# Selective scan over 128 x 128 pixels: middle-group rows stored in turn, and the carried state added to the first token instead of being the scan's initial value

## The chip, the cores and the metric

One core of one Trainium2 chip. The metric is the device time of one execution in microseconds (us); the time before is the median of three runs. Where a profile is read, it is that of one profiled execution, whose own time stands beside it.

## The reference, cut to what matters

Two images of 96 channels and 128 x 128 pixels go through a layer norm, a four-directional selective scan (Mamba), a feed-forward part with 8-bit rounding, a 3 x 3 convolution and a second feed-forward part. Nearly all the time goes to the scan, which for each of four pixel orders (rows, rows backwards, columns, columns backwards) computes:

```python
xz = x @ in_w.T
xc, z = jnp.split(xz, 2, axis=-1)            # 192 channels each
xc = silu(causal_conv4(xc) + conv_b)
xdbl = xc @ xproj_w.T                        # dt (6), B (16), C (16) per token
dt = softplus(dt_raw @ dt_w.T + dt_b)
A = -jnp.exp(A_log)                          # 192 channels x 16 states
# for every token, in order:
dA = jnp.exp(dt_t[:, :, None] * A)
h = dA * h + dt_t[:, :, None] * B_t[:, None, :] * u_t[:, :, None]
y = jnp.einsum('bds,bs->bd', h, C_t)
# then
y = (y + Dp * xc) * silu(z)
out = y @ outp_w.T                           # and a fusion of the four orders
```

## The kernel before, in words

For each image, `normalize` writes the normed image to DRAM once by rows (`xnr`) and once by columns (`xnc`). `mamba` then does the scans, and `ffn_and_conv` the rest.

**Tiling of the scan.** Two pixel orders are worked together as a pair (`PAIRS`: rows with columns, then the two backward ones). 2 x 192 channels make three groups `g` of 128 partitions. Group 1, the middle one, holds the last 64 channels of the first order on partitions 0 to 63 and the first 64 of the second order on 64 to 127. The 16384 tokens are cut into 32 pieces of 512 (`T`). A pair and a piece are a step (`pi`, `i`): 64 steps per image, 128 in all. A step has 24 units: three groups times eight pairs of states (`s`, `s + 1`). A unit `k` is handled in turn `k` of one loop (L436), which writes out the order of every engine's instructions by hand:

- `fetch` (L386) loads, every second turn, B rows six turns and C rows four turns ahead (`B_AHEAD`, `C_AHEAD`), on SyncE's queue (SP). `row_tile` (L312) copies each row from DRAM to all partitions of the group: 1 MB a tile in one transfer, but for the middle group in two of 512 KB, 64 partitions each, since the two orders have different rows.
- `feed` (L391) multiplies the B rows with dt times u on GpSimd (`b_part`, L324), two units ahead; `feed_decay` makes `exp(dt A)` on ScalarE into PSUM (`decay`, L330), two units ahead.
- `scan` (L334) runs the recurrence on VectorE, one instruction per state, written over the decay in PSUM. Its initial value is the number 0 in a first piece (`i == 0`), else a column of `hst`. The order within a turn is: first scan of unit k, `behind(k - 1)`, second scan of unit k.
- `behind` (L403) multiplies with the C rows on VectorE (L409), copies the last state to `hst` on ScalarE (L410), and sums over states on TensorE into PSUM `y` (`sums`, L341). When a group begins, the `y` of the last one is gated (`gated`, L349, VectorE).
- The next step's `prologue` (L210) is spread over the turns by a list `at` (L301) of turn, place in the turn and function: input loads in turn 0, input convolutions on TensorE in turns 4, 5 and 6 with ScalarE taking the results in the same turns (L233), the gates in 7, 10 and 11, silu of xc at the end of turn 8 and of sz at the end of turn 14 (`silu`, L244, with a table load on either side), the B, C and dt rows in turn 12, from where they are stored to DRAM (L261). The softplus of each group starts in turns 13, 18 and 21 and takes four GpSimd operations (L287, L290, L293, L297).
- `project` and `collect` (L352, L361) apply the output weights (`gmat`) four turns after a group ends, that is, in turn 3 of the next step for the last group.

All engines keep this order; SP's transfers wait in it too, each for the buffer that it writes. A B tile has four buffers, a C tile three, the decay three.

`_layout` (L566) rearranges the weights on the host.

Of the kernel before, what the change touches and what calls it, by code (L numbers as in the profile page):

```python
# [10 lines left out]
F32 = mybir.dt.float32  # L11
# [9 lines left out]
C = 96  # L21
# [21 lines left out]
def tile_metaformer(ctx: ExitStack, tc: tile.TileContext, a: dict, out: bass.AP):  # L43
# [34 lines left out]
    inx = cpool.tile([C, 4, 4, DI], F32, name="inx")  # L78
    nc.vector.memset(gmat, 0.0)
    with tc.tile_pool(name="prep", bufs=1) as pp, tc.tile_pool(name="prep_ps", bufs=2, space=PSUM) as pps:  # L80
        alog = pp.tile([128, 2, NG, S], F32, name="alog")
        nc.sync.dma_start(alog, a["alog"])
        nc.scalar.activation(alog, alog, AF.Exp)
        nc.vector.tensor_scalar_mul(amat, alog, -1.0)

        dskip = pp.tile([128, 2, NG], F32, name="dskip")
        nc.sync.dma_start(dskip, a["dskip"])
        for pi in range(2):
            for g in range(NG):
                nc.vector.tensor_scalar_mul(dmat[:, pi, g, :], ident, dskip[:, pi, g : g + 1])  # L90

        inxw = pp.tile([C, 4, DI], F32, name="inxw")
        nc.sync.dma_start(inxw, a["inx"])
        taps = pp.tile([C, 4, 4, DI], F32, name="taps")
        nc.sync.dma_start(taps, a["taps"].broadcast_to((C, 4, 4, DI)))
        for d in range(4):
            nc.vector.tensor_tensor(inx[:, d], taps[:, d], inxw[:, d, None, :].broadcast_to((C, 4, DI)), ALU.mult)
        outw = pp.tile([C, 4, DI], F32, name="outw")
        nc.sync.dma_start(outw, a["outw"])
        fusew = pp.tile([C, 4, C], F32, name="fusew")  # L100
        nc.sync.dma_start(fusew, a["fusew"])
        for pi, (da, db) in enumerate(PAIRS):

            pieces = [
                (slice(0, 128), da, 0, 128),
                (slice(0, 64), da, 128, 192),
                (slice(64, 128), db, 0, 64),
                (slice(0, 128), db, 64, 192),
            ]
            for g, (rows, d, lo, hi) in enumerate(pieces):  # L110
                ps = pps.tile([128, C], F32, name="ps")
                nc.tensor.matmul(ps[rows, :], outw[:, d, lo:hi], fusew[:, d, :], start=True, stop=True)
                nc.vector.tensor_copy(gmat[rows, pi, g, :], ps[rows, :])

# [68 lines left out]
    def mamba(acc, xnr, xnc):  # L183

        with ExitStack() as st:
# [4 lines left out]

            hst = one.tile([128, NG, S], F32, name="hst")
            acc_w = acc.rearrange("c (h w) -> c w h", w=W)

# [16 lines left out]
            def prologue(pi, i, d):  # L210
# [19 lines left out]
                def conv_out(g):  # L230
                    if g == 0:
                        d["xc"] = two.tile([128, NG, T], F32, name="xc")
                    nc.scalar.activation(d["xc"][:, g, :], d["ps"], AF.Identity, bias=convb[:, pi, g : g + 1])  # L233

# [3 lines left out]
                def gate_out(g):  # L238
                    if g == 0:
                        d["sz"] = two.tile([128, NG, T], F32, name="sz")  # L240
                    nc.scalar.copy(d["sz"][:, g, :], d["ps"])

# [12 lines left out]
                def rows_out():  # L255

                    d["rows"] = one.tile([BCO + NBC, T], F32, name="rows")
                    nc.scalar.copy(d["rows"], d["ps"][0 : BCO + NBC, :])
                    d["bcd"] = rows_d.tile([COPIES, 2, NBC // 2, T], F32, name="bcd")
                    for n in range(COPIES):  # L260
                        nc.sync.dma_start(d["bcd"][n].rearrange("k r t -> (k r) t"), d["rows"][BCO:, :])  # L261
# [39 lines left out]
                at = [(0, 0, load), (8, 1, partial(silu, "xc")), (14, 1, partial(silu, "sz"))]  # L301
                at += [(12, 0, rows), (12, 1, rows_out)]
                for g, k in enumerate((4, 5, 6)):
# [8 lines left out]
            def row_tile(d, g, s, k, ahead):  # L312

                t = gen.tile([128, 4, T], F32, name=f"row{k}", bufs=ahead + 1)
                for half in range(2) if g == 1 else (slice(None),):
                    rows = slice(half * 64, half * 64 + 64) if g == 1 else half
                    at = s + S * (half if g == 1 else g // 2)
                    n = (64 if g == 1 else 128) // COPIES
                    src = d["bcd"][None, :, k, at : at + 4, :].broadcast_to((n, COPIES, 4, T))
                    nc.sync.dma_start(t[rows], src)  # L320
                return t

            def b_part(d, g, b):
                nc.gpsimd.tensor_tensor(b, d["dtu"][g][:, None, :].broadcast_to((128, 2, T)), b, ALU.mult)  # L324

            def decay(pi, d, g, s):
# [5 lines left out]

            def scan(i, g, s, j, da, b, h):
                nc.vector.tensor_tensor_scan(  # L334
                    h[:, j, :], da[:, j, :], b[:, j, :],
                    0.0 if i == 0 else hst[:, g, s + j : s + j + 1], ALU.mult, ALU.add,
                )

# [52 lines left out]
            def feed(k):  # L391
                if k < total:
                    n = k // nu
                    b_part(state[n], units[k % nu][0], bs[k])

# [40 lines left out]
            for k in range(total + 6):  # L436
                n, u = divmod(k, nu)
                if u == 0 and n + 1 < len(steps):
                    for m, where, f in prologue(*steps[n + 1], state[n + 1]):
                        later(k + m, where, f)  # L440
                if k % 2 == 0:
                    fetch(k + 2 * B_AHEAD, 0, B_AHEAD, bs)
                feed(k + AHEAD)
                issue(k, 0)
                if k < total:
                    (_, i), (g, s) = steps[n], units[u]
                    da, b = das.pop(k), bs.pop(k)
                    hs[k] = b if (g, s) in BY_POOL else da
                    scan(i, g, s, 0, da, b, hs[k])
                if 0 < k <= total:  # L450
                    behind(k - 1)
                if k < total:
                    scan(i, g, s, 1, da, b, hs[k])
                if k % 2 == 0:
# [111 lines left out]
def _layout(v):  # L566

    f = np.float32
    order = [d for pair in PAIRS for d in pair]
    rows = lambda w: w[order].reshape(2, NG, 128, -1).transpose(2, 0, 1, 3)  # L570
    xw = v["L0_conv_xproj_w"]
    bcw = np.zeros((2, 2 * DI, BCO + NBC), f)
    dtw = np.zeros((2 * RK, 2, 2 * DI), f)
    for pi, pair in enumerate(PAIRS):
        for k, d in enumerate(pair):
# [5 lines left out]
            dtw[k * RK : (k + 1) * RK, pi, at] = v["L0_conv_dt_w"][d].T  # L581
    grouped = lambda w: w.reshape(2, NG, 128, -1).transpose(2, 0, 1, 3)
    out = {
# [4 lines left out]
        "taps": v["L0_conv_conv_w"].transpose(0, 2, 1)[None],  # L588
        "convb": rows(v["L0_conv_conv_b"])[..., 0],
        "bcw": grouped(bcw),  # L590
        "dtw": dtw,
        "dtb": rows(v["L0_conv_dt_b"])[..., 0],
        "alog": rows(v["L0_conv_A_log"]),
        "dskip": rows(v["L0_conv_Dp"])[..., 0],
        "outw": v["L0_conv_outp_w"].transpose(1, 0, 2),
        "fusew": v["L0_conv_fuse_w"].reshape(C, 4, C).transpose(2, 1, 0),
# [26 lines left out]
```

## Time and profile before

| | |
|---|---|
| median of three runs | 13000.71 us (12998.91 to 13001.96) |
| profiled execution | 13004.29 us, span of its core 13002.5 us |
| granted TensorE clock, mean | 0.963 of full speed |
| VectorE scans (L334) | 6144 of some 1.27 us, 7565 us busy |
| GpSimd B multiplies (L324) | 3072 of 2.36 us, 7176 us busy |
| ScalarE decays (L330) | 6144 of 0.69 us, 4249 us busy |
| TensorE sums over states (L341) | 12288 passes, 6120 us busy |
| VectorE C multiplies (L409) | 3072 of 1.21 us, 3706 us busy |
| transfers | 3400 MB, 262 GB/s over the span |

The profile is one execution, recorded by the chip. Each row of instruction groups gives line, engine, operation, the tiles that it writes and reads with their shapes, and the count; then busy time in us, the mean duration of one in ns, and how long the engine stood idle just before them, with what ended that idle time. In rows in order of time the first number is the start in us, the second the duration of the merged instructions, and brackets hold the idle time before them and what ended it. TensorE is PE (PEld its weight loads), VectorE DVE, ScalarE ACT, GpSimd POOL, SyncE's queue SPq. The releaser in brackets is inferred; where several things were waited for, only the last is named.

### The profile page before, as it was taken

The page shows a single profiled execution, that of the slowest core. Times are in us where ns is not written, and L with a number is a line of the kernel's source. Part 1 is how long each engine was busy: PE and PEld are TensorE (multiplying, and loading weights), DVE is VectorE, ACT ScalarE, POOL GpSimd, SP SyncE. Part 2 cuts the span into 40 slices and gives each one's busy share as a digit, 9 for nine tenths or more (in the row PEclk, how much of TensorE's full clock was granted, in tenths as well). Part 3 has the DMA queues.
Part 4 walks back from the last instruction along what each step waited for, and adds up shares of the span by engine and source line. Part 5 has one row for each costly group of instructions (what it writes and reads, how often), then busy time and mean ns, then how long its engine had stood idle before and what let it go on. Part 6 is the DMA issues. An engine that isn't in the chain of part 4 may idle for free. (4 is left out here: it accounts for less than half of the span.)

```text
span 13002.5 us, 97992 instructions
## 1 busy us (share of the span) xinstructions
PE 10850.3 (83%) x24208; PEld 3987.1 (31%) x24208; DVE 11569.1 (89%) x10865; ACT 8560.0 (66%) x14738; POOL 9215.4 (71%) x4772
## 2 busy tenths in 40 slices
PE   6888888888888888888978888888888888888889
PEld 2323233333333333333323333332333333333233
DVE  5999999999999999995459999999999999999954
ACT  6666666666666666665566666666666666666655
POOL 4877778777787787772147778777787777877721
PEclk8999999999999999999989999999999999999999
DMA  7999999999999999992079999999999999999920
GB/s 226 287 294 282 298 288 285 295 283 298 288 285 295 283 295 289 285 295 68 13 226 285 298 283 292 290 285 298 285 291 291 284 298 286 290 294 281 296 61 13
DMA packets 545331, 3400.40 MB, mean 262 GB/s; under 512 B 81612, under 2 KB 82732, under 8 KB 146840
## 3 DMA queue, kind: packets, MB, share of 16 engines
q1 hardware_dynamic: 544760, 3394.12, 83.1%
q8 instruction: 195, 3.19, 0.1%
q14 instruction: 376, 3.08, 0.1%
HBM read 3288.94 MB, written 104.86 MB: 261 GB/s over the span
## 5 line engine op out<-in xcount | busy, mean ns | idle before, releaser
L324 POOL TENSOR_TENSOR row<-dtu,row 128x1024 f32<-128x1024 f32 x3072 | 7175.7, 2358 | 1739.3 <-DMA row<-bcd 1419.2
L334 DVE TENSOR_TENSOR_SCAN da<-da,hst,row 128x512 f32<-128x512 f32 x5952 | 7339.4, 1274 | 351.2 <-ACT da L330 194.6
L341 PE MATMUL y<-row,ident 128*128 128x512 f32 x12288 | 6120.1, 626 | 1113.3 <-DVE row L409 1098.9
L330 ACT ACTIVATE da<-dt,amat 128x512 f32<-128x512 f32 x6144 | 4249.4, 692 | 207.5 <-ACT hst L410 0.4
L341 PEld LDWEIGHTS y<-row,ident 128*128 128x128 f32 x12288 | 2288.9, 197 | 4779.4 <-DVE row L409 2292.3
L409 DVE TENSOR_TENSOR row<-da,row 128x1024 f32<-128x1024 f32 x3072 | 3705.9, 1206 | 19.6 <-DMA row<-bcd 18.8
L410 ACT COPY hst<-da 128x2 f32<-128x2 f32 x3072 | 484.0, 158 | 2235.5 <-DVE row L409 2233.3
L416 PE MATMUL y<-xc,dmat 128*128 128x512 f32 x768 | 526.1, 773 | 779.1 <-DVE sz L349 779.1
L287 POOL TENSOR_TENSOR q<-e,q 128x512 f32<-128x512 f32 x384 | 488.0, 1271 | 821.8 <-ACT hst L410 709.1
L233 ACT ACTIVATE xc<-misc,convb 128x512 f32<-128x512 f32 x384 | 264.2, 688 | 1117.5 <-PE misc L207 1117.5
L207 PE MATMUL misc<-xa,inx 96*128 96x512 f32 (+1 forms) x2048 | 932.4, 597 | 59.0 <-DMA xa<-xnr 57.2
L207 PE MATMUL misc<-xb,inx 96*64 96x512 f32 (+1 forms) x2048 | 928.1, 595 | 1.6 <-ACT xc L233 1.6
L531 POOL TENSOR_TENSOR acc<-acc,y 96x512 f32<-96x512 f32 x128 | 147.6, 1153 | 987.0 <-DVE y L530 987.0
L541 PE MATMUL pc<-pad,kw 96*96 96x512 f32 x1152 | 566.7, 593 | 0.0
L207 PEld LDWEIGHTS misc<-xa,inx 96*128 96x128 f32 (+1 forms) x2048 | 323.6, 163 | 625.5 <-issue 493.4
L293 POOL TENSOR_TENSOR dt<-dt,ln 128x512 f32<-128x512 f32 x384 | 486.9, 1268 | 30.1
L297 POOL TENSOR_TENSOR dtu<-dt,xc 128x512 f32<-128x512 f32 x384 | 488.5, 1272 | 0.5
L290 POOL TENSOR_TENSOR ln<-ln,q 128x512 f32<-128x512 f32 x384 | 488.1, 1271 | 0.5
L359 PE MATMUL misc<-sz,gmat 128*96 128x512 f32 x1024 | 483.6, 594 | 0.0
L416 PEld LDWEIGHTS y<-xc,dmat 128*128 128x128 f32 x768 | 129.0, 211 | 1102.1 <-DVE sz L349 1099.1
L268 PE MATMUL misc<-rows,dtw 12*128 12x512 f32 x768 | 439.7, 652 | 18.5 <-ACT dt L275 17.2
L132 DVE TENSOR_TENSOR xq<-xm,rs 96x512 fp8e5<-96x512 f32 x128 | 87.9, 687 | 387.8 <-ACT rs L128 387.8
(75 smaller groups left out, 8403.8 us busy)
## 6 DMA issues: line engine op xcount, KB each, us to landing
row<-bcd SPq DMA_DIRECT2D x2048, 1024.0 KB, 7.5
row<-bcd SPq DMA_DIRECT2D x2048, 512.0 KB, 8.0
bcd<-rows SPq DMA_DIRECT2D x512, 128.0 KB, 9.8
xa<-xnr SPq DMA_DIRECT2D x124, 193.1 KB, 5.8
xb<-xnc SPq DMA_DIRECT2D x124, 193.1 KB, 5.5
acc<-in_x_dram SPq DMA_DIRECT2D x16, 768.0 KB, 17.8
xnr<-xn SPq DMA_DIRECT2D x16, 768.0 KB, 4.3
xnc<-stg SPq DMA_DIRECT2D x16, 768.0 KB, 5.6
```

The source lines that it names most:

```text
L207: nc.tensor.matmul(ps[rows, :], w(PAIRS[pi][d], k, lo, hi), src[d][:, k : k + T], **se)
L287: nc.gpsimd.tensor_tensor(d["q"], d["e"], d["q"], ALU.subtract)
L290: nc.gpsimd.tensor_tensor(d["ln"], d["ln"], d["q"], ALU.add)
L293: nc.gpsimd.tensor_tensor(d["dt"][g], d["dt"][g], d["ln"], ALU.add)
L297: nc.gpsimd.tensor_tensor(dtu, d["dt"][g], d["xc"][:, g, :], ALU.mult)
L324: nc.gpsimd.tensor_tensor(b, d["dtu"][g][:, None, :].broadcast_to((128, 2, T)), b, ALU.mult)
L330: nc.scalar.activation(da[:, j, :], d["dt"][g], AF.Exp, scale=amat[:, pi, g, s + j : s + j + 1])
L334: nc.vector.tensor_tensor_scan(h[:, j, :], da[:, j, :], b[:, j, :], 0.0 if i == 0 else hst[:, g, s + j : s + j + 1], ALU.mult, ALU.add,)
L341: nc.tensor.matmul(y, ident, c[:, j, :], start=False, stop=s + j == S - 1)
L409: nc.vector.tensor_tensor(c, h, c, ALU.mult)
L416: nc.tensor.matmul(y, dmat[:, pi, g, :], d["xc"][:, g, :], start=True, stop=False)
L541: nc.tensor.matmul(pc, kw[:, t, :], rows, start=t == 0, stop=t == 8)
```

## The change

Three things are changed.

**Rows of the middle group in turn.** In group 1 the 64 channels of the first order now lie on the even partitions and those of the second on the odd ones. `row_tile` writes every second partition in each of its two transfers. TensorE still produces the two halves on partitions 0 to 63 and 64 to 127; ScalarE takes them into a tile of their own (`mixed`), and two transfers of 64 x 512 elements each (`mix`), issued on SP, move them to every second row of `xc` (turn 7) and of `sz` (turn 12). The silu of turns 8 and 14 reads what they wrote. The weights are rearranged to match, those for the output with zero rows in between (`outx`), so that `gmat` needs no memset.

**The state enters through the first token.** All scans start from the number 0. Instead, for steps with `i > 0`, `entering` makes `exp(dt A)` of a group's first token for its 16 states on ScalarE and multiplies it with `hst` on GpSimd (128 x 16), at the end of turn 20 for group 0, and of turns 4 and 12 of the step itself for groups 1 and 2. `b_part` then adds two of these values to the first tokens of the unit's B tile, an operation of 128 x 2 elements on GpSimd after the multiply.

**Row stores later.** The copies of the B and C rows to DRAM are issued at the start of turn 14 instead of the end of turn 12 (`rows_to_dram`).

```diff
                 def conv_out(g):
                     if g == 0:
                         d["xc"] = two.tile([128, NG, T], F32, name="xc")
-                    nc.scalar.activation(d["xc"][:, g, :], d["ps"], AF.Identity, bias=convb[:, pi, g : g + 1])
+                    t = mixed("xc") if g == 1 else d["xc"][:, g, :]
+                    nc.scalar.activation(t, d["ps"], AF.Identity, bias=convb[:, pi, g : g + 1])
...
-                    nc.scalar.copy(d["sz"][:, g, :], d["ps"])
+                    nc.scalar.copy(mixed("sz") if g == 1 else d["sz"][:, g, :], d["ps"])
+
+                def mixed(name):
+                    d["mix", name] = one.tile([128, T], F32, name=f"mix_{name}")
+                    return d["mix", name]
+
+                def mix(name):
+
+                    for k in range(2):
+                        nc.sync.dma_start(d[name][k:128:2, 1, :], d["mix", name][64 * k : 64 * k + 64, :])
...
-                at += [(12, 0, rows), (12, 1, rows_out)]
+                at += [(12, 0, rows), (12, 1, rows_out), (14, 0, rows_to_dram)]
+                at += [(7, 0, partial(mix, "xc")), (12, 0, partial(mix, "sz"))]
...
-                    rows = slice(half * 64, half * 64 + 64) if g == 1 else half
+
+                    rows = slice(half, 128, 2) if g == 1 else half
...
-            def b_part(d, g, b):
+            def entering(pi, d, g):
+
+                nc.scalar.activation(enter[:, g, :], amat[:, pi, g, :], AF.Exp, scale=d["dt"][g][:, 0:1])
+                nc.gpsimd.tensor_tensor(enter[:, g, :], enter[:, g, :], hst[:, g, :], ALU.mult)
+
+            def b_part(i, d, g, s, b):
                 nc.gpsimd.tensor_tensor(b, d["dtu"][g][:, None, :].broadcast_to((128, 2, T)), b, ALU.mult)
+                if i > 0:
+                    nc.gpsimd.tensor_tensor(b[:, :, 0], b[:, :, 0], enter[:, g, s : s + 2], ALU.add)
...
-            def scan(i, g, s, j, da, b, h):
-                nc.vector.tensor_tensor_scan(
-                    h[:, j, :], da[:, j, :], b[:, j, :],
-                    0.0 if i == 0 else hst[:, g, s + j : s + j + 1], ALU.mult, ALU.add,
-                )
+            def scan(j, da, b, h):
+                nc.vector.tensor_tensor_scan(h[:, j, :], da[:, j, :], b[:, j, :], 0.0, ALU.mult, ALU.add)
...
                     for m, where, f in prologue(*steps[n + 1], state[n + 1]):
                         later(k + m, where, f)
+                    if steps[n + 1][1] > 0:
+                        for g in range(NG):
+                            later(k + nu - 4 + nu // NG * g, 1, entering, steps[n + 1][0], state[n + 1], g)
```

## The prediction, made before the changed kernel ran

> **What bounds the kernel now.** I read the engine totals first, then busy time by stage, then the groups with shapes kept apart, then VectorE, GpSimd, ScalarE and SyncE in order of time through one step. The chain of waits is no help: it covers only the last few per cent. The two scan stages (168 to 5936 us and 6650 to 12427 us) hold 11,545 of the 13,002 us; each is 64 steps of 24 units, so a step takes some 90 us.
>
> ```profile
> PE 10850.3 (83%) x24208; PEld 3987.1 (31%) x24208; DVE 11569.1 (89%) x10865; ACT 8560.0 (66%) x14738; POOL 9215.4 (71%) x4772
> ...
> row<-bcd SPq DMA_DIRECT2D x2048, 1024.0 KB, 7.5
> row<-bcd SPq DMA_DIRECT2D x2048, 512.0 KB, 8.0
> ```
>
> VectorE leads. The 512 KB transfers (half a middle-group tile) take as long to land as whole tiles. By stretches (PE, PEld, DVE, ACT, POOL busy, then clock, DMA share, GB/s):
>
> ```profile
> 2924.00:2934.00 10.00, 6.19 (x13) 2.04 (x13) 9.76 (x9) 9.56 (x14) 2.65 (x2) 1.00 1.00 388
> 2984.00:2994.00 10.00, 10.00 (x29) 4.13 (x26) 8.51 (x8) 4.34 (x9) 6.39 (x4) 1.00 0.82 197
> ```
>
> Middle-group transfers move half the bytes per second. The second stretch is also one where PE is full and VectorE is not. The scans, by shape:
>
> ```profile
> L334 DVE TENSOR_TENSOR_SCAN da<-da,hst,row 128x512 f32<-128x512 f32 x5952 | 7339.4, 1274 | 351.2 <-ACT da L330 194.6 <-ACT hst L410 134.2 <-issue 21.2
> ...
> L334 DVE TENSOR_TENSOR_SCAN da<-da,row 128x512 f32<-128x512 f32 x192 | 225.6, 1214 | 180.9 <-POOL row L324 170.9 <-ACT hst L410 5.2 <-ACT da L330 4.7
> ```
>
> The 192 scans of the four first steps already take a constant as initial value: 60 ns shorter. One step, VectorE:
>
> ```profile
> 2990.84 1.28 DVE L334 TENSOR_TENSOR_SCAN da<-da,hst,row 128x512 f32<-128x512 f32 x1
> 2993.61 1.29 DVE L334 TENSOR_TENSOR_SCAN da<-da,hst,row 128x512 f32<-128x512 f32 x1 [1.49 <-ACT da L330]
> ...
> 3024.90 1.29 DVE L334 TENSOR_TENSOR_SCAN da<-da,hst,row 128x512 f32<-128x512 f32 x1 [1.27 <-ACT hst L410]
> ```
>
> A unit (two scans, one multiply) repeats every 3.486 us; a gating (L349) adds 0.6. Twice per step VectorE waits for ScalarE: at unit 9 and at unit 17. GpSimd, ScalarE and SyncE around these:
>
> ```profile
> 3023.38 1.27 POOL L287 TENSOR_TENSOR q<-e,q 128x512 f32<-128x512 f32 x1 [5.28 <-ACT hst L410]
> ...
> 3061.60 18.60 POOL L324 TENSOR_TENSOR row<-dtu,row 128x1024 f32<-128x1024 f32 x8
> ```
> ```profile
> 2991.32 0.69 ACT L233 ACTIVATE xc<-misc,convb 128x512 f32<-128x512 f32 x1 [3.15 <-PE misc L207]
> ...
> 2996.02 1.28 ACT L244 ACT_TABLE_LOAD   x1
> 2997.31 1.48 ACT L244 ACTIVATE xc<-xc 128x1536 f32<-128x1536 f32 x1
> ```
> ```profile
> 2993.03 1.15 SPq L320 DMA_DIRECT2D row<-bcd  x2
> ```
>
> From the first L287 of a step (3023.38; the one before stands at 2933.50, so 89.88 us apart) GpSimd runs without a gap until 3080.2. And from the multiply of unit 1 (ends 2970.0) PE runs without a gap through projection, three input convolutions and the sums, until ScalarE can take the last convolution at 2991.32; decay of unit 9 and its scan (2993.61) follow. So a step is a relay: GpSimd's run, then PE's, then VectorE, then ScalarE to the next L287. VectorE's 89% hides that.
>
> [...]scans (decay in PSUM, b in SBUF) stay within 1257 to 1293 ns, so the added GpSimd work does not stretch VectorE's. [...]
>
> **The change part by part.**
>
> *Scans without a state pointer.* 0.060 us each, 0.12 per unit (3.486 to 3.366), 2.88 per step, 357 us over 124 steps with i > 0, if VectorE set the pace throughout. It does so only from unit 9 to unit 14: there 5 x 0.12 = 0.6 us is saved. Before unit 9 PE sets it, from unit 14 to 17 ScalarE (silu, logarithm). The four constant-start steps bear this out: L287 to L287 across the one at 3050 is 3023.38 to 3113.26, 89.88 us, no shorter than its neighbour.
>
> *The GpSimd adds.* 24 per step, 128x2, each waiting for the multiply before it; no such row exists. GpSimd's 512-element operations start 1.225 us apart, the 1024-element ones 2.31: 2.12 ns an element and 0.14 fixed. An operation that waits for its predecessor starts 0.12 later (L290 to L293: 1.35). Sum 0.27 us. Ends: 0.10 (a memset of 3 columns takes 98 ns, no wait) and 0.50; a gain is excluded, since work is only added. The three 128x16 multiplies cost 0.2 and may wait for their Exp on ScalarE (free for this one by the times below); behind them stand the next units' multiplies, for which the scans wait.
> Time from a step's first L287: unit 17 scans at 1.52 (3024.90). VectorE alone would reach unit 1 at 1.52 + 8 x 3.366 + 0.6 = 29.05. GpSimd ended unit 1's multiply at 28.58 (3051.96); eight adds and one multiply make it 28.58 + 8 x 0.27 + 0.2 = 30.94. So VectorE waits, is at unit 2 at 31.0 + 3.97 = 35.0, against 34.1 now (2967.6 - 2933.5): 0.9 us lost. From there to unit 9 is PE's 26.0 us (2967.6 to 2993.61), before and after; GpSimd's later lag (unit 4 at 43.7) fits in it. With the ends of the add: -0.5 (29.6 at unit 1) to +2.7 (32.8).
>
> *Rows in turn.* [...]middle-group tiles should load in 2.6 us, not 5. No scan waits for a row load in a running step, so the direct gain is nothing.
>
> *The mixing DMAs.* Four per step, 128 KB each. The pair for xc stands on SP behind the two c loads of units 10 and 11, which wait for PE's sums of unit 5; these end at 2993.0, and the loads issue at 2993.03. So the pair issues at 2994.2 and 2994.8. Data start 1.2 us after issue (the DMA share is zero until 2994.2); the c tile ahead needs 2.6 us, to 2996.8; the pair[...] 1.3 us[...]: landed at 2998.8. The silu's table load, which now waits for it, wants to start at 2996.02. ScalarE stands 2.8 us; queued behind are silu, table load, hst copy and the decay of unit 11, 5.7 us in all: 2998.8 + 5.7 = 3004.5. VectorE wants unit 11 at 2993.61 + 2 x 3.366 + 0.6 + 1.4 (gating waits for PE) = 3002.3. Loss 2.2; I take 2.1. Ends: 1.3 if the data reach full rate, 4.7 if alternate rows load no faster.
> Each pair also sets SP's next loads back by 1.2 us: b of unit 14 is wanted 15 us later, free. The pair for sz issues near 3007.5 and lands near 3013, the silu starts at 3017.18: free. Without that cover it would stall like xc.
>
> *The rest.* Three Exps of 128x16 (some 0.2) fall where ScalarE waits 1 to 3 us anyway; the one at unit 20 has 1.0 us before the scan. Row stores two units later: four issues of 0.6 us past one b load of SP; landing 9.8 us later, near 3028, before the first reader (3029.17): free, though with 1 us. Preparation: a memset of 0.7 us less, a larger weight load: nothing.
>
> *Sum.* -0.6 + 0.9 + 2.1 = 2.4 us per step. 124 x 2.4 = 298, two more steps with the mixing wait alone, 4. The profiled execution took 13004.3 (span 13002.5), 3.6 above the median of the runs: 13000.7 + 302, say 13300.
>
> **Rivals.**
> A, the forecast: both waits as priced, 13300, own range 13120 to 13450. Chance 0.55.
> B, slower still: the c tile ahead of the mixing pair loads no faster, so xc lands 2.5 us later, -0.6 + 0.9 + 4.7 = 5.0 per step: 13620. For it: two 64-row transfers remain two. [...]Chance 0.15.
> C, faster: the xc pair is hidden. The DMA engines stand idle from 2992.4 to 2994.2; if it lands by 2996.6, 0.6 after the table load wants to start, ScalarE recovers before unit 11. With adds of 0.10 to 0.15 unit 2 is reached at 33.6 to 34.0, 0.5 to 0.1 early: with the 0.6 that is -1.1 to -0.7 per step, 12865 to 12915. For it: a pair is small, 256 KB. Against: the c megabyte stands ahead. Chance 0.22.
> D, they cancel: adds of 0.15 and a wait of 1.1: 13000, within 0.2%. Chance 0.08.
> That a scan would not shorten is excluded by the 192 constant ones.
>
> **How the numbers follow.** 0.2% (26 us) is about what a measurement of this kernel can tell. Faster 0.22, same 0.08, slower 0.70. From 12860 to 13620 holds A, C, D and the near half of B; what is left out is a larger gain (VectorE alone setting the pace, 12650) or a larger loss.
>
> **What would show it.** Right: scans at 1.21 us, middle-group stretches near 390 GB/s; L287 to L287 near 92 us; scans at units 19 to 4 waiting for GpSimd's added operations; the table load ahead of the silu of xc waiting 2 to 3 us for xc<-mix. Wrong: no wait at that table load, adds under 0.15 us, or unit 9 reached in less than 26 us from unit 2.

## The result and the profile after

The changed kernel takes 13828.95 us, median of four runs (13827.55 to 13831.25), against 13000.49 us for the kernel before, run in turn with it on the same chip: a ratio of 1.0637, with a 95% interval of 1.0619 to 1.0656. The span of its profiled execution is 13825.8 us, that of before 13002.5: 823 us more, or some 6.6 us for each of the 124 steps with a carried state. The mean granted TensorE clock fell from 0.963 to 0.931.

Line numbers are each kernel's own. In the kernel after, L349 is the scan, L345 the decay, L337 the B multiply, L339 the add, L353 the sums, L421 the C multiply, L422 the copy to `hst`, L201 the input products, L236 the copy of a gate out of PSUM, L245 the mixing transfers, L248 the silu with the table load before it, and L255 and L261 the B, C and dt rows on TensorE and their copy out of PSUM.

The same rows of the page as before, in the kernel after. In a group's row the last part is the idle time of the engine just before these instructions and what ended it; the last three rows give KB of a transfer and us from issue to landing.

```profile
PE 11090.9 (80%) x24208; PEld 4131.6 (30%) x24208; DVE 11297.2 (82%) x10864; ACT 8653.6 (63%) x15110; POOL 9825.5 (71%) x8120
...
L349 DVE TENSOR_TENSOR_SCAN da<-da,row 128x512 f32<-128x512 f32 x6144 | 7298.2, 1217 | 1642.1 <-ACT hst L422 948.5
...
L339 POOL TENSOR_TENSOR row<-row,enter 128x2 f32<-128x2 f32 x2976 | 574.4, 193 | 233.3
L248 ACT ACT_TABLE_LOAD x256 | 328.4, 1283 | 635.0 <-DMA xc<-mix_xc 629.0
...
row<-bcd SPq DMA_DIRECT2D x2048, 1024.0 KB, 6.9
row<-bcd SPq DMA_DIRECT2D x2048, 512.0 KB, 7.5
...
xc<-mix_xc SPq DMA_DIRECT2D x256, 128.0 KB, 6.0
```

The scans became shorter, 1217 ns against 1274, and VectorE is busy 272 us less. But it now waits more before its scans, 1642 us in place of 532 (351.2 and 180.9), and most of that is for ScalarE. ScalarE in turn waits where it never did: 629.0 us before the table load of the silu, for `xc<-mix_xc`, which is 5.0 us in each of 126 steps. And the 512 KB transfers still land no sooner than the 1024 KB ones (7.5 against 6.9 us), although their rows now lie in turn.

Three stretches of a step in which middle-group tiles are loaded; the columns are those of the stretches shown before (busy us of PE, PEld, DVE, ACT, POOL, then clock, DMA share, GB/s).

```profile
2495.00:2505.00 10.00, 10.00 (x30) 3.95 (x30) 9.68 (x9) 6.40 (x12) 9.69 (x10) 1.00 0.76 210
2505.00:2515.00 10.00, 10.00 (x30) 4.04 (x27) 8.85 (x9) 4.49 (x9) 9.69 (x9) 1.00 0.81 197
2515.00:2522.00 7.00, 6.21 (x16) 2.38 (x16) 5.62 (x6) 2.26 (x5) 4.63 (x4) 1.00 1.01 245
```

They move 210, 197 and 245 GB/s; the stretch of before that the prediction showed moved 197. In the first two, as in that one, the DMA engines are not busy all the time (shares 0.76 and 0.81, and 0.82 there), so that these are not rates of a transfer; in the third they are, and 245 is far from the 388 of whole tiles. Alternate rows bring no speed that could be seen here; the loads by themselves, below, measure it.

Now one step in order of time, engine by engine. VectorE first: the first scans of units 11 and 17.

```profile
2527.33 1.23 DVE L349 TENSOR_TENSOR_SCAN da<-da,row 128x512 f32<-128x512 f32 x1 [3.94 <-ACT hst L422]
...
2551.69 1.23 DVE L349 TENSOR_TENSOR_SCAN da<-da,row 128x512 f32<-128x512 f32 x1 [4.06 <-ACT hst L422]
```

SyncE's queue and ScalarE around these two waits:

```profile
2515.14 1.18 SPq L245 DMA_DIRECT2D xc<-mix_xc  x2
```
```profile
2521.53 1.28 ACT L248 ACT_TABLE_LOAD   x1 [4.67 <-DMA xc<-mix_xc]
2522.82 1.48 ACT L248 ACTIVATE xc<-xc 128x1536 f32<-128x1536 f32 x1
...
2525.62 0.16 ACT L422 COPY hst<-da 128x2 f32<-128x2 f32 x1
...
2528.70 0.58 ACT L236 COPY mix_sz<-misc 128x512 f32<-128x512 f32 x1
...
2537.91 0.58 ACT L261 COPY rows<-misc 96x512 f32<-96x512 f32 x1 [3.00 <-PE misc L255]
...
2543.97 1.28 ACT L248 ACT_TABLE_LOAD   x1
```

TensorE in the same stretch, and a stretch of 6 us behind its idle time:

```profile
2522.72 1.98 PE L353 MATMUL y<-row,ident 128*128 128x512 f32 x4
2529.33 2.07 PE L201 MATMUL misc<-xb,inz 96*128 96x512 f32 x2 [4.62 <-ACT mix_sz L236]
2531.20 3.62 PE L353 MATMUL y<-row,ident 128*128 128x512 f32 x4
2534.61 3.26 PE L255 MATMUL misc<-xc,bcw 128*96 128x512 f32 x6
```
```profile
2529.00:2535.00 6.00, 5.67 (x7) 2.41 (x8) 6.00 (x6) 4.18 (x9) 0.01 (x1) 0.50 1.01 296
```

The reader is to see one wait run through three engines. The pair for xc is issued at 2515.14, and ScalarE goes on at 2521.53, 6.4 us later. Behind the silu stand the decays that the scan of unit 11 needs: VectorE waits 3.94 us. (The brackets name the copy to `hst` beside these decays; the scans here read no `hst`, and the decay of unit 11 ends at 2527.2.) Behind it, too, stands the copy that empties the gate's PSUM tile (`mix_sz`, 2528.70); the next gate on TensorE needs that tile and waits 4.62 us, and because TensorE keeps its order, the sums behind it and the B, C and dt rows (L255) come late as well. They come later still because the clock that TensorE was granted right behind this idle time was 0.50: four passes of sums took 3.62 us there, and 1.98 before. ScalarE then waits 3.00 us for those rows, reaches the silu of sz at 2543.97, and VectorE waits a second time, at unit 17. The lower clock belongs to this place: between units 11 and 16 it was 0.84 of full speed, as a mean over 116 steps, against 1.00 in the kernel before.

To put numbers on this, the time from a unit's first scan to the next unit's first scan was averaged over those 116 steps, whose piece is neither of the first two nor the last of a pair:

| from unit to unit | before, us | after, us | difference | by the prediction's terms |
|---|---|---|---|---|
| 17 to 2 of the next step | 32.60 | 33.39 | +0.79 | +0.9 |
| 2 to 9 | 26.33 | 26.69 | +0.36 | 0 |
| 9 to 10 | 5.53 | 5.46 | -0.07 | -0.12 |
| 10 to 11 | 3.49 | 7.73 | +4.24 | +2.1 - 0.12 |
| 11 to 16 | 17.62 | 16.85 | -0.77 | -0.36 |
| 16 to 17 | 4.67 | 6.73 | +2.06 | 0 |
| sum | 90.24 | 96.84 | +6.60 | +2.4 |

Each figure is rounded by itself. 124 steps times 6.60 us are 818 of the 823 us.

### The profile page after: what moved, and what is told of

Same layout as the page of the kernel before. It is cut to its first block, busy times and chain, and to the rows that moved or that the text cites. A ratio compares the mean times of both kernels' runs of the same rounds, so it can differ in the third digit from the quotient of the medians.

```text
span 13825.8 us, 102488 instructions
## 1 busy us (share of the span) xinstructions
PE 11090.9 (80%) x24208; PEld 4131.6 (30%) x24208; DVE 11297.2 (82%) x10864; ACT 8653.6 (63%) x15110; POOL 9825.5 (71%) x8120
## 3 DMA queue, kind: packets, MB, share of 16 engines
q14 instruction: 411, 3.36, 0.1%
## 5 line engine op out<-in xcount | busy, mean ns | idle before, releaser
L349 DVE TENSOR_TENSOR_SCAN da<-da,row 128x512 f32<-128x512 f32 x6144 | 7298.2, 1217 | 1642.1 <-ACT hst L422 948.5
L337 POOL TENSOR_TENSOR row<-dtu,row 128x1024 f32<-128x1024 f32 x3072 | 7230.7, 2355 | 886.5 <-DMA row<-bcd 877.5
L353 PE MATMUL y<-row,ident 128*128 128x512 f32 x12288 | 6250.0, 640 | 821.2 <-DVE row L421 820.8
L345 ACT ACTIVATE da<-dt,amat 128x512 f32<-128x512 f32 x6144 | 4249.1, 692 | 199.2 <-ACT hst L422 0.2
L353 PEld LDWEIGHTS y<-row,ident 128*128 128x128 f32 x12288 | 2387.8, 203 | 4536.6 <-issue 2624.4
L421 DVE TENSOR_TENSOR row<-da,row 128x1024 f32<-128x1024 f32 x3072 | 3707.1, 1207 | 0.1
L422 ACT COPY hst<-da 128x2 f32<-128x2 f32 x3072 | 482.1, 157 | 2199.4 <-DVE row L421 2178.6
L201 PE MATMUL misc<-xa,inx 96*128 96x512 f32 (+1 forms) x2048 | 942.6, 602 | 100.1 <-DMA xb<-xnc 56.0
L201 PE MATMUL misc<-xb,inx 96*64 96x512 f32 (+1 forms) x2048 | 928.1, 595 | 1.6 <-ACT mix_xc L228 1.6
L201 PE MATMUL misc<-xb,inz 96*64 96x512 f32 (+1 forms) x512 | 396.2, 866 | 629.6 <-ACT mix_sz L236 629.6
L339 POOL TENSOR_TENSOR row<-row,enter 128x2 f32<-128x2 f32 x2976 | 574.4, 193 | 233.3
L248 ACT ACT_TABLE_LOAD x256 | 328.4, 1283 | 635.0 <-DMA xc<-mix_xc 629.0
L334 POOL TENSOR_TENSOR enter<-enter,hst 128x16 f32<-128x16 f32 x372 | 82.3, 221 | 744.1 <-ACT enter L333 743.7
L201 PEld LDWEIGHTS misc<-xa,inx 96*128 96x128 f32 (+1 forms) x2048 | 316.4, 163 | 699.4 <-issue 467.6
L228 ACT ACTIVATE xc<-misc,convb 128x512 f32<-128x512 f32 x256 | 176.0, 687 | 529.6 <-PE misc L201 529.6
```

What stands on the lines that cost most here:

```text
L201: nc.tensor.matmul(ps[rows, :], w(PAIRS[pi][d], k, lo, hi), src[d][:, k : k + T], **se)
L339: nc.gpsimd.tensor_tensor(b[:, :, 0], b[:, :, 0], enter[:, g, s : s + 2], ALU.add)
L345: nc.scalar.activation(da[:, j, :], d["dt"][g], AF.Exp, scale=amat[:, pi, g, s + j : s + j + 1])
L349: nc.vector.tensor_tensor_scan(h[:, j, :], da[:, j, :], b[:, j, :], 0.0, ALU.mult, ALU.add)
L353: nc.tensor.matmul(y, ident, c[:, j, :], start=False, stop=s + j == S - 1)
L421: nc.vector.tensor_tensor(c, h, c, ALU.mult)
```

## The experiments

The theory after this reading: the rows in turn cost nearly everything, through the wait for the mixing pair, which is long because a tile of alternate rows loads no faster than one of adjacent rows; the wait at unit 17 is its echo. The state entry alone costs about what the prediction priced. Rivals: that the adds on GpSimd are the cost, that the added traffic of the mixing is, or that a TensorE held back by its clock is. Unless something else is said, ratios are to the kernel before, run in turn on the same chip. It took 13004.03 us beside four of the kernels (the xc pair earlier, rows alone, entry alone, constant scans), 13000.22 beside three (both pairs earlier, and the entry with a later silu, without and with the earlier projection) and 12998.71 beside two (the later silu without the entry, without and with the earlier projection).

### The xc pair one turn earlier

```diff
-                at += [(7, 0, partial(mix, "xc")), (12, 0, partial(mix, "sz"))]
+                at += [(6, 0, partial(mix, "xc")), (12, 0, partial(mix, "sz"))]
```

> The changed kernel with the xc pair of mixing transfers issued at the start of turn 6, ahead of the two C loads, instead of turn 7; nothing else differs. If the wait for this pair is the main cost (unit 10 to 11 takes 7.73 us instead of 3.49, unit 16 to 17 6.73 instead of 4.67), both intervals go back and the time falls by 126 x (4.3 + 2.1) = 805 us, to 13020. If the adds on GpSimd are the main cost, it falls by less than 250 us. If slower row loads are the cost, it stays at 13830.

Measured: 13540.70 us (13530.67 to 13551.45), ratio 1.0413 (1.0397 to 1.0428). A miss by 520 us. The first wait is gone indeed: unit 10 to 11 is 3.36 us. But the wait has moved to the other pair (the waits of the kernel, total, times, longest):

```profile
ACT L248 <- DMA sz<-mix_sz: 481.4, 126, 6.3
```

The pair for sz, which waited 3.7 us in all in the kernel after, now holds ScalarE 3.8 us in each step, and unit 16 to 17 takes 8.52 us. So the sz pair was not free in itself. It was covered by the delay that the xc pair caused. The prediction had said that without cover it would stall like xc; it does.

### Both pairs earlier

```diff
-                    if g == 0:
+                    if "sz" not in d:
...
-                at += [(7, 0, partial(mix, "xc")), (12, 0, partial(mix, "sz"))]
+                at += [(6, 0, partial(mix, "xc")), (8, 0, partial(mix, "sz"))]
...
-                for g, k in enumerate((7, 10, 11)):
+                for g, k in ((1, 7), (0, 10), (2, 11)):
```

The gate of the middle group is made first, so that its data are there to be mixed at turn 8.

> The kernel e1 with the pair for sz early too: the gate of the middle group is made in turn 7 instead of 10, and its mixing pair issued at the start of turn 8 instead of 12. In e1 the silu of sz waits for it and unit 16 to 17 takes 8.52 us. If waits for mixing pairs are all that rows in turn cost, the time falls to that of the state entry alone: 13066 (within 13040 to 13100). If rows in turn cost something else, it stays above 13150.

Measured: 13114.92 us (13110.16 to 13118.56), ratio 1.0089 (1.0072 to 1.0105), 714 us below the kernel after. That is 15 us above the range of the theory (13040 to 13100) and below what anything else was to cost (more than 13150): nearly all, but not quite all, was waits for mixing pairs. The silu's table load no longer waits:

```profile
L248 ACT ACT_TABLE_LOAD x256 | 328.4, 1283 | 4.5
```

Units 10 to 11 take 3.36 us and 16 to 17 take 4.52, below the 4.67 of before. All rows still lie in turn, all four mixing transfers are still made and all adds too. So the traffic and the layout as such are cheap. With the first wait the second is gone too, and the mean granted clock of the execution is 0.958, against 0.931 in the kernel after, as befits an echo. 49 us remain above the state entry alone (next but one). Nearly all of them lie in one place: unit 9 to 10 takes 5.81 us in place of 5.47, because VectorE's gating waits longer for TensorE's sums (221.9 us in all, 180.0 there). With the xc pair alone moved it took 5.46. So this wait came with the second part of this edit, the sz pair and the exchanged gates, and not with the rows.

### Rows in turn alone

The kernel after with its scans started from `hst` as before, and without `entering` and the adds.

```diff
-                if i > 0:
-                    nc.gpsimd.tensor_tensor(b[:, :, 0], b[:, :, 0], enter[:, g, s : s + 2], ALU.add)
...
-                nc.vector.tensor_tensor_scan(h[:, j, :], da[:, j, :], b[:, j, :], 0.0, ALU.mult, ALU.add)
+                nc.vector.tensor_tensor_scan(
+                    h[:, j, :], da[:, j, :], b[:, j, :],
+                    0.0 if i == 0 else hst[:, g, s + j : s + j + 1], ALU.mult, ALU.add,
+                )
```

> The changed kernel with rows in turn and mixing transfers, but the scans with the state as initial value and no adds on GpSimd. If the mixing wait is the main cost: 13000 + 126 x (4.3 + 2.1) = 13806, nearly the changed kernel. If the adds are: near 13050.

Measured: 13679.05 us (13674.50 to 13680.63), ratio 1.0519 (1.0503 to 1.0534). Its table load waits as in the kernel after, without a single add on GpSimd:

```profile
L247 ACT ACT_TABLE_LOAD x256 | 328.4, 1283 | 630.0 <-DMA xc<-mix_xc 627.5
```

Unit 10 to 11 takes 7.65 us and 16 to 17 takes 6.38. The theory had priced 13806, 127 us more; the two waits are somewhat shorter here, and unit 2 to 9 takes 26.00 us, 0.33 less than before. That the adds were the main cost is out: 675 of the 828 us come with the rows alone. And that a slower TensorE is what lengthens unit 2 to 9 is out as well, for the mean clock is as low here as in the kernel after (0.932), and this stretch is shorter.

### The state entry alone

The kernel before with `entering`, the adds and constant scans, and its own rows in two halves.

```diff
+                if i > 0:
+                    nc.gpsimd.tensor_tensor(b[:, :, 0], b[:, :, 0], enter[:, g, s : s + 2], ALU.add)
...
-                nc.vector.tensor_tensor_scan(
-                    h[:, j, :], da[:, j, :], b[:, j, :],
-                    0.0 if i == 0 else hst[:, g, s + j : s + j + 1], ALU.mult, ALU.add,
-                )
+                nc.vector.tensor_tensor_scan(h[:, j, :], da[:, j, :], b[:, j, :], 0.0, ALU.mult, ALU.add)
```

> The kernel before with the state entering through the first token (adds on GpSimd, scans from a constant), rows of the middle group as before and no mixing transfers. If the mixing wait is the main cost: units 17 to 9 some 1.1 us longer, 9 to 17 some 0.8 shorter, so 13000 + 124 x 0.3 = 13040, within 12950 to 13130. If the adds are the main cost: near 13800. If VectorE set the pace all through: 12640 and what the adds cost.

Measured: 13065.66 us (13064.12 to 13072.61), ratio 1.0049 (1.0034 to 1.0064): the prediction's terms without the mixing, -0.6 + 0.9, give 13040. Its scans:

```profile
L342 DVE TENSOR_TENSOR_SCAN da<-da,row 128x512 f32<-128x512 f32 x6144 | 7275.9, 1216 | 799.0 <-POOL row L332 395.2 <-POOL row L330 176.6 <-ACT da L338 117.7
```

VectorE saves 60 ns a scan and gives it back waiting for the adds (L332), 395.2 us in all. Unit 17 to 2 takes 33.33 us, about as in the kernel after, and unit 2 to 9 takes 26.76: the lengthening of both belongs to the state entry.

### Constant scans, the state dropped

The kernel before with every scan started from 0 and no state carried over, which leaves a part of the computation out.

```diff
-                    0.0 if i == 0 else hst[:, g, s + j : s + j + 1], ALU.mult, ALU.add,
+                    0.0, ALU.mult, ALU.add,
```

> The kernel before with every scan starting from the constant 0: the state is dropped from piece to piece, so part of the computation is left out; nothing is added to GpSimd. This prices the shorter scans alone. If a step is a relay of GpSimd, PE, VectorE and ScalarE: 9 units before PE's run and 5 after it gain 0.12 us each, 124 x 1.7 = 210, 12790. If VectorE sets the pace: 357 less, 12643. If the four constant first steps are typical: no gain, 13000.

Measured: 12813.13 us (12812.30 to 12815.55), ratio 0.9853 (0.9837 to 0.9870). The relay that the prediction described was to give 12790, VectorE alone 12643. So the shorter scans are worth 191 us (13004.03 - 12813.13) in this order of work, not the 357 of all scans times 60 ns. Against the run before, everything that brings the state in costs 13065.66 - 12813.13 = 252.5 us, 2.0 per step.

### Loads by themselves

Nothing of the reference is computed here, and the output is zeros. Twelve tiles of 1 MB are loaded in each of several ways into three buffers; a small VectorE copy marks the landing of each of the last three. The transfers that a tile is made of, in short:

```python
t[64 * h : 64 * h + 64]          # halves: two of 64 adjacent rows
t[h:128:2]                       # turns: two of 64 alternate rows
t[:, 2 * h : 2 * h + 2, :]       # columns: two of 128 rows, half as wide
t[h:128:2, 0, :] <- full[64 * h : 64 * h + 64, 0, :]    # mixes: the pair of 128 KB
```

> None of the reference is computed (the output is zeros); the kernel only loads 12 tiles of 1 MB each, in four ways one after the other: in one transfer to 128 partitions; in two to 64 neighbouring partitions each; in two to every second partition; in two to 128 partitions with half the columns; then 12 times the mixing pair. If [...]as the forecast assumed, the third way takes 2.6 us a tile like the first, and the second 5. If [...](the middle-group stretches of the changed kernel show 197 to 210 GB/s), the third takes 5 like the second. If two transfers as such are slow, the fourth takes 5 too. The mixing pair alone should take 1.3 us or less.

The last mark of each way (of turns the last two), in order of time; in brackets the wait since the mark before it:

```profile
42.43 0.15 DVE L64 COPY mark<-t_whole 128x1 f32<-128x1 f32 x1 [2.31 <-DMA t_whole<-bcd]
...
100.95 0.15 DVE L64 COPY mark<-t_halves 128x1 f32<-128x1 f32 x1 [4.40 <-DMA t_halves<-bcd]
...
154.40 0.15 DVE L64 COPY mark<-t_turns 128x1 f32<-128x1 f32 x1 [4.38 <-DMA t_turns<-bcd]
158.62 0.15 DVE L64 COPY mark<-t_turns 128x1 f32<-128x1 f32 x1 [4.07 <-DMA t_turns<-bcd]
...
194.24 0.15 DVE L64 COPY mark<-t_columns 128x1 f32<-128x1 f32 x1 [2.34 <-DMA t_columns<-bcd]
...
212.04 0.15 DVE L64 COPY mark<-t_mixes 128x1 f32<-128x1 f32 x1 [1.14 <-DMA t_mixes<-full]
```

From the start of one mark to the next, averaged over the last three marks of each way: 2.5 us for a whole tile, 4.6 for halves, 4.4 for turns, 2.5 for columns, and 1.3 for a mixing pair. Alternate rows load at 239 GB/s (1.049 MB in 4.38 us), hardly above the 229 of adjacent ones. Two transfers are not slow because they are two (columns); what the two slow ways share is that each transfer has 64 rows. The pair itself costs the 1.3 us that the prediction gave it.

The traces of the two kernels agree. The two halves of the C tile that the pair stands behind land 4.6 and 6.3 us after the issue of each in the step shown above, as alternate rows. In the step of before that the prediction shows, as adjacent rows (issued at 2993.03), they land after 4.8 and 6.7 us.

### More ways to load 64 and 64 rows

Again loads alone, output zeros: halves and turns with their two transfers on the queues of SyncE and ScalarE, and tiles in four transfers of 32 rows, adjacent or every fourth. In the first line `q` is SyncE's queue for one half and ScalarE's for the other.

```diff
+            q.dma_start(t[64 * h : 64 * h + 64], v)
...
+            load(t[32 * p : 32 * p + 32], 32, k, s + 16 * (p % 2))
...
+            load(t[p:128:4], 32, k, s + 16 * (p % 2))
```

> Loads by themselves, nothing of the reference is computed and the output is zeros: 12 tiles of 1 MB in each way. The run before had, per tile, 2.5 us in one transfer, 4.6 us as two halves of 64 adjacent rows, 4.4 us as two halves of 64 alternate rows. If what limits is each transfer's own partitions: halves on two queues run side by side and take 2.5 to 3 us. If [...]: two queues stay above 4 us. Quarters of 32 adjacent rows, and quarters of every fourth row, in one queue: above 4.4 us if each transfer is bound by its own partitions and they run one after another, near 2.5 us if several in flight share the work.

Measured per tile, in the same way: halves on two queues 4.1 us, turns on two queues 4.4, quarters of adjacent rows 4.95, of every fourth row 6.3. No way comes near 2.5, and two queues stay above 4 us: that each transfer's own partitions set the rate, so that two run side by side, is out (halves take 4.1 us on two queues, and 4.6 on one in the run before). One tile of alternate rows in this run came 9.4 us after the one before it; no other did, and it was not followed.

### The stride alone: thirds

Loads alone once more, output zeros. Is a transfer of fewer than 128 rows slow as such, or does the stride of its rows count? In halves it changed little (4.6 and 4.4 us a tile), in quarters more (4.95 and 6.3). Here a tile of 126 rows is loaded in three transfers of 42, of adjacent rows or of every third row: the number of rows and of transfers stays, and only the stride differs.

```diff
+        nc.sync.dma_start(dst, bcd[None, 0:3, k, at : at + 4, :].broadcast_to((14, 3, 4, T)))
...
+            third(t[42 * p : 42 * p + 42], k, s + 8 * p)
...
+            third(t[p:126:3], k, s + 8 * p)
```

> Loads by themselves, nothing of the reference is computed and the output is zeros; per tile of 1 MB, the mean of the last two of twelve. Controls: one transfer 2.5 us, two of alternate rows 4.4 to 4.6 us. New: three transfers of 42 rows each (126 rows), of adjacent rows and of every third row. Theory 1, [...]a tile takes 3 us or less; 42 adjacent rows [...]4.5 us or more. Theory 2, a transfer of fewer than 128 rows is slow as such, whatever its rows: both take 4.5 us or more.

```profile
164.63 0.15 DVE L66 COPY mark<-t_thirds_adjacent 126x1 f32<-126x1 f32 x1 [5.45 <-DMA t_thirds_adjacent<-bcd]
170.04 0.15 DVE L66 COPY mark<-t_thirds_adjacent 126x1 f32<-126x1 f32 x1 [5.26 <-DMA t_thirds_adjacent<-bcd]
...
211.42 0.15 DVE L66 COPY mark<-t_thirds_every_third 126x1 f32<-126x1 f32 x1 [3.30 <-DMA t_thirds_every_third<-bcd]
214.77 0.15 DVE L66 COPY mark<-t_thirds_every_third 126x1 f32<-126x1 f32 x1 [3.19 <-DMA t_thirds_every_third<-bcd]
```

Three transfers of every third row take 3.4 us a tile (1.03 MB, 303 GB/s), three of adjacent rows 5.5 (188 GB/s); alternate rows took 4.5 in the same run and a whole tile 2.5. Same bytes, same number of transfers and rows in each, another stride: 1.6 times as fast. That a transfer of fewer than 128 rows is slow as such, whatever its rows, is out. The DMA engines were about as busy both times: in fortieths of the span that hold one way alone, but for the last, the page counts eight or nine tenths for each, at 175 to 191 GB/s for adjacent rows and at 292 to 324 for every third row.

So the stride counts, but for less than the first theory's 3 us for every third row, which was the author's estimate. And a wider stride is not faster in every case: in the run before, quarters of every fourth row took 6.3 us and those of adjacent rows 4.95. By what the stride changes the rate was not shown by any run here, and the cause of the slow alternate rows stays open.

### The state entry with a later silu

The last runs ask whether the state entry can pay. On ScalarE the silu of sz (two table loads and 1.48 us) stands at the end of turn 14, right beside a softplus; the scan of unit 17 waits behind both. The edit moves it two turns on.

```diff
-                at = [(0, 0, load), (8, 1, partial(silu, "xc")), (14, 1, partial(silu, "sz"))]
+                at = [(0, 0, load), (8, 1, partial(silu, "xc")), (16, 1, partial(silu, "sz"))]
```

First on top of the state entry alone:

> The state entry alone (e2) with the silu of sz at the end of turn 16 instead of 14, so that ScalarE reaches the first logarithm some 4 us sooner and GpSimd starts its run some 4 us sooner. If GpSimd's run from the first L287 to unit 4 is what the adds cost (2.0 us a step), this cost and the wait at units 15 to 17 go: 13066 - 124 x 2.0 - 126 x 1.7 = 12600, within 12550 to 12720. If the adds cost otherwise: 12850 and more.

Measured: 12727.92 us (12714.04 to 12737.04), ratio 0.9789 (0.9774 to 0.9804), 8 us above the range. Then, as its counterpart, the kernel before with this edit alone:

> The kernel before, with only the silu of sz moved from the end of turn 14 to the end of turn 16; states stay initial values, no adds. If the state entry pays once the late silu no longer holds up the step: the kernel with both takes 88.14 us per step; without the adds some 2.0 less, with 24 units of scans that are 0.12 longer each some 2.9 more, so about 89.1 us against 90.24, 128 x 1.1 = 145 us: 12855 (12780 to 12930), above the 12728 of the kernel with both. If the entry is worth nothing and all of that gain is the later silu's: 12728 or less.

Measured: 12850.28 us (12832.69 to 12861.67), ratio 0.9888 (0.9872 to 0.9905); 12855 (12780 to 12930) was expected of an entry that pays. Unit 16 to 17 takes 3.48 us in place of 4.67. In the kernel with the state entry the scans are 1214 ns long and wait for the adds 238.9 us (395.2 with the silu in its old place):

```profile
L342 DVE TENSOR_TENSOR_SCAN da<-da,row 128x512 f32<-128x512 f32 x6144 | 7219.3, 1214 | 530.6 <-POOL row L332 238.9 <-POOL row L330 174.5 <-ACT da L338 116.0
```

In the kernel without it they keep 1268 ns, hardly wait, and GpSimd stands idle 1885 us before its multiplies, mostly for row tiles:

```profile
L334 DVE TENSOR_TENSOR_SCAN da<-da,hst,row 128x512 f32<-128x512 f32 x5952 | 7303.9, 1268 | 208.5 <-ACT da L330 192.8 <-issue 10.2 <-POOL row L324 5.4
L324 POOL TENSOR_TENSOR row<-dtu,row 128x1024 f32<-128x1024 f32 x3072 | 7172.1, 2356 | 1885.0 <-DMA row<-bcd 1548.1 <-DVE row L409 304.4 <-DVE da L334 31.4
```

So the state entry alone costs 62 us, the later silu alone gains 148, and both together gain 272, not 87. Once the silu no longer holds back the relay, VectorE sets the pace from unit 16 to the end of the step (3.48 us a unit without the entry, 3.36 with it), and there the shorter scans count. Not all of it is gained: at units 2 and 3 the scans still wait for the adds (4.91 and 3.80 us). What remains is 12850 - 12728 = 122 us.

### Projection one turn earlier

On both of these, `project` and `collect` behind the last group one turn earlier (for the middle group, `g == 1`, they stay):

```diff
-                    later(k + 4, 0, project, pi, i, d, g)
-                    later(k + 4, 1, collect, pi, d, g)
+                    at = k + 4 if g == 1 else k + 3
+                    later(at, 0, project, pi, i, d, g)
+                    later(at, 1, collect, pi, d, g)
```

With the state entry and the later silu:

> The kernel e7 with the output projection of the last group one turn earlier (turn 2 of the next step instead of 3), so that PE's run before unit 9 starts with 1.7 us less behind it. If PE's run sets the arrival at unit 9 (intervals 7 to 9 hold some 3.5 us of waits), some 1.5 us a step more go: 190 below e7, near 12410. If not, as e7.

Measured: 12654.41 us (12650.91 to 12665.96), ratio 0.9735 (0.9720 to 0.9749), the fastest of all: 2.7% below the kernel before and 8.5% below the kernel after. But only 73 us came of this edit, where 190 were expected. Unit 8 to 9 went from 4.48 to 3.85 us, still above 3.36; what holds it there was not followed further.

With the later silu alone:

> The kernel before, with the silu of sz at the end of turn 16 and projection and collection of the outer groups one turn earlier, without the state entry. If the entry pays: some 1.0 us per step above the 87.47 of the kernel that has it, 12780 (12720 to 12850). If it is worth nothing: 12654 or less.

Measured: 12829.75 us (12821.57 to 12834.52), ratio 0.9869 (0.9854 to 0.9884). This is within the range of an entry that pays. The gain is 21 us here, less than the 29 us between the fastest and the slowest run without this edit: 8 to 9 went from 5.16 to 4.77 us, while 7 to 8, 15 to 16 and 17 to 18 grew. With the earlier projection in both, the state entry is worth 175 us.

## Why the prediction was wrong: point by point

- **Slower, and how.** The direction was right, and so were the relay of engines and the place of the main wait, the table load before the silu of xc. The size was not: +6.6 us per step in place of +2.4, and 13829 lies above the whole range.
- **Shorter scans.** 1217 ns against 1274: right. From unit 9 on each interval without a wait fell from 3.49 to 3.36 us, as said. It lasted to unit 16 and not to 14 only, which gave 0.4 us more, because VectorE was behind.
- **The adds.** 0.27 us was taken. Multiplies with an add between them start 2.58 us apart in the median, without one 2.31: 0.27. Unit 17 to 2 lost 0.79 us, 0.9 was said. The state entry alone gave 13066 for a priced 13040.
- **Unit 2 to 9, PE's own time.** Said to be the same, with GpSimd's lag fitting in it; 0.36 us longer. The lag does not quite fit. The scans of units 2 and 3 are held up by the adds (4.95 and 3.81 us, 3.49 each before), the sums come later, and TensorE, which had no gap between units 4 and 9 before, stands idle for 0.35 us there. The clock is not the reason: it was 1.00 there (the stretches above), and the time is 26.76 us with the state entry alone, 26.00 with the rows alone.
- **Rows in turn: the step that failed.** "middle-group tiles should load in 2.6 us, not 5." This rate of alternate rows was the author's estimate, and the step failed at it: the loads alone show 4.4 us. The direct gain was put at nothing; since no load got faster, no run tests that. But the same 2.6 us stood in the price of the mixing pair, behind the c tile. With 4.4 the working reads so: issue to ScalarE's start was said to be 2998.8 - 2994.2 = 4.6 us, and 1.8 more is 6.4. The trace shows 2521.53 - 2515.14 = 6.4; that it fits to a tenth is partly luck, since a part of that sum, what follows the data of the pair up to its landing, was an estimate that no trace showed, and over all steps 2.8 + 1.8 = 4.6 stands against a mean wait of 5.0. Unit 10 to 11 lost 4.24 us where the sum had 2.1 - 0.12. The edit that issues the xc pair earlier takes it away from the C tile and from SyncE's wait for that tile's buffer at once; that the 1.8 us are the tile's load rate rests on the loads alone and on the landings. Rival B had named this mechanism and priced the wait's loss at 4.7; its chance of 0.15 was too low, since the slow landing of two 64-row transfers was in the trace and the full rate of alternate rows was in none. (The 197 GB/s shown for them is not half the rate of whole tiles: at a DMA share of 0.82 it is some 240 while the engines are busy, and by themselves adjacent halves load at 229 GB/s and whole tiles at 416, 1.049 MB in 2.52 us.)
- **The second wait: the step that was missing.** "From unit 14 to 17 ScalarE" sets the time, with or without the change, and so the sum had nothing there. 16 to 17 lost 2.06 us. The prediction followed the late ScalarE to the decay of unit 11 and stopped. It did not ask what else stood behind the silu: the copy that empties the gate's PSUM tile, for which TensorE waits, and with TensorE the rows, the softplus and the second silu; nor that TensorE would be granted half its clock behind such idle time (0.50 in the 6 us shown above). With both pairs early, idle time, low clock and second wait go together, so that the share of the clock in the 2.06 us stays open.
- **The sz pair: "free".** So it was, but only behind the other wait. With the xc pair early it cost 3.8 us per step.
- **The rest** (Exp of 128 x 16, 0.29 us each where some 0.2 was said, row stores, preparation) shows no cost: with both pairs early the whole change stands 49 us above the state entry alone, and nearly all of that is the gating's wait that came with that edit.
- **A sum that does not come out.** Rival D, adds of 0.15 and a wait of 1.1, gives -0.6 - 0.15 + 1.1 = +0.35 us per step by the prediction's own terms, 43 us and not within 26. It decides nothing here.

From these terms the 828 us (13828.95 - 13000.49) divide so: 62 belong to the state entry (13065.66 - 13004.03), 49 remain with the mixing out of the way (13114.92 - 13065.66), and 714 to the waits for the mixing pairs (13828.95 - 13114.92); 3 us lie between the runs of the kernel before. What stays open is the part of TensorE's lower clock in the 714, and why alternate rows load slowly.

## What to carry to other kernels

Before you price a wait, list every instruction queued behind it on its engine, the copies that free a PSUM tile for another engine among them, and follow each to its own reader: here the same wait came due twice in a step. A term that rests on a rate no trace has shown belongs in the range with its worst value, and where it stands in a second term too, it must be moved there as well. And a shortening off the path can be worth keeping: try it again together with the removal of what held the path, since the two gains are not a sum (62 lost alone, 122 gained behind the later silu).

## What the runs showed of the hardware that was not expected

- The stride of the rows that a transfer writes changes its rate at the same number of rows: 126 rows in three transfers took 5.5 us as adjacent rows and 3.4 us as every third row, and 64 alternate rows, spread over the whole height, were as slow (4.4 us a tile) as 64 adjacent ones (4.6).
- A tile in two transfers of 128 rows and half the width takes 2.5 us, like one transfer. Splitting by columns cost nothing; every way of splitting by rows that was tried did (3.4 us at best).
- A GpSimd addition of 128 x 2 elements takes 193 ns, and some 0.27 us of its engine's time from start to start when it waits for the operation before it.
- Behind 4.62 us of idle time TensorE was granted 0.50 of its clock for the next 6 us of the trace, and four passes of sums took 3.62 us in place of 1.98. The mean clock of the whole execution, 0.931, does not show where this falls.
